# Last image's loads with channels outermost, the second softmax term cast by GpSimd, and scores brought onto pixels by transposes

## The chip, the cores and the metric

The kernel runs on one core of one Trainium2 chip. The metric is device time in microseconds of one execution. Before the change the median of three runs is 5360.88 us (5352.83 to 5364.77).

A core has five engines that run their own instruction queues in order and wait for each other by semaphores: TensorE (PE, with its weight loads listed as PEld), VectorE (DVE), ScalarE (ACT), GpSimd (POOL) and SyncE (SP), which here only issues transfers. TensorE writes to PSUM[...].

## The reference, cut to what matters

The input x is 16 images of 56 x 56 pixels and 384 channels, float32. Two layers follow each other:

```python
x = x + _L0_conv_ref(_gn(x), w_qkv, w_proj, b_proj)   # dilated attention
x = x + _L1_conv_ref(_gn(x), w_conv)                  # depthwise 3x3, binary weights
```

`_gn` is a group norm over 32 groups of 12 channels and a whole image. The attention computes q, k and v with one 384 x 1152 product, and cuts them into 3 groups of 128 channels with dilations 1, 2 and 3. Each group has 4 heads of 32 channels. A pixel attends to its 3 x 3 neighbours at that dilation (9 taps): q times k summed over a head's 32 channels gives 3 x 4 x 9 = 108 scores a pixel, a softmax runs over the 9 taps, and the weights multiply v. A 384 x 384 product and the residual follow. The second layer convolves each channel by itself with weights -1, 0 or 1.

## The kernel before, in words

**Tiling.** An image is cut into 7 chunks of 8 rows, 448 pixels (`PX`), so there are 112 chunks. Inside the kernel a tile holds 128 channels on the partitions and 448 pixels along the free dimension. Images pass through DRAM between stages, channels first: `xd` (the input, transposed) and `x1d` (after the attention).

**Stages.** `plan_a` loads a chunk, transposes it on TensorE (L422), takes statistics and stores it to `xd`. `plan_b` is the attention of one chunk: `normalise`, `k_or_v` and `query` (L463), `score`, the softmax, `turn_weights`, `weigh`, `out_project`. `plan_c` is the convolution and the output of one chunk.

**Order of the work.** The pieces of all plans are entered with `at(when, order, piece)` and then called sorted by time slot and by kind. A chunk advances by `STEP` = 9 slots, so pieces of several chunks and images interleave. The tile framework then schedules the instructions engine by engine, sets the semaphores and gives out the buffers of the pools; nothing else orders the queues. Almost all transfers are issued on SP's queue, in order.

**Scores to softmax.** `score` multiplies q with three shifted copies of k on VectorE (L516, tile `t`). `score_rounds` sums each head's 32 channels by products with a 0/1 matrix (L501), into the PSUM tile `ps`: 27 rounds of 4 rows at scattered places. `softmax_1` copies `ps` to `sT` (ACT, L533) and brings it onto pixels with four matmuls, one for each 112 pixels (L536): `sT` is the stationary operand and `permf`, a 128 x 128 matrix of zeros and ones built at the start (L107), the moving one. It orders the columns by neighbour, and columns 108 to 127 come out as zeros, since only 27 x 4 of its entries are set. Maximum, difference and exponential (L541 to L543), sum, reciprocal and product (L547 to L549) follow.

**Three terms.** The weights `ew` are float32. To carry them through a bfloat16 transposing transfer without loss, they are split in three bfloat16 terms, written in place into `e3`: the first is a cast (ACT, L558), `rest` is what the cast lost (POOL, L559), the second a cast of `rest` (ACT, L563), the third what that lost (POOL, L564). `turn_weights` issues the transposing transfer into `aT` on SP (L569). `weigh` spreads the three terms over the channels by bfloat16 products (L582, tile `pb_a`), VectorE multiplies with v (L589, tile `w`), GpSimd adds up the taps (L597, L600, L601, tiles `w` and `y`), and `out_project` takes `y` through TensorE (L615, tile `po`).

**The last image's convolution.** Its chunks (b = B-1) have no later attention beside them. `load` (L684, L692) fills, for each of two channel groups j, four sets q of 32 channels, each three times on the partitions with rows shifted by one (ky = 0, 1, 2): 96 partitions. The tiles come from the pools `t`, `w` and `xr`, two sets in a tile. For the chunks 1 to 5 one transfer for each q brings all three shifts:

```python
one = by_set[:, q, p0 - W : p0 - W + PX]
three_rows = bass.AP(one.tensor, one.offset, [(W, 3), *one.ap])
nc.sync.dma_start(set_of(j, q), three_rows)
```

The edge chunks 0 and 6, and all other images, use one transfer for each ky (L684). `normalise` (L699, L703) follows, then `convolve` (L717, L724) and `taps_last` (L759), the third group's nine taps on VectorE. `turn` transposes the result (L789), copies it to `osb` (L791, pool `o_p`, two buffers) and stores it (L794), for the last image from ACT's queue.

Of the kernel before, what the change touches and what calls it, by code (L numbers as in the profile page):

```python
# [8 lines left out]
F32 = mybir.dt.float32  # L9
# [8 lines left out]
P = 128  # L18
HEADS = 4
HD = 32  # L20
NG = 3
NTAP = 9
NQ = 4
ROWS = 8
SUB = 112
# [3 lines left out]
NPAD = 32  # L29
# [6 lines left out]
def dilated_attention_then_binary_conv(  # L36
# [28 lines left out]
    nc = tc.nc  # L65
    B, H, W, C = x.shape
    PX = ROWS * W
    NCH = H // ROWS
# [7 lines left out]
    def place(p):  # L76

        g, o = divmod(p, NTAP)
        return NG * o + g
# [22 lines left out]

    perm = const.tile([P, NPAD, HEADS], F32, name="perm")
    nc.gpsimd.memset(perm, 0.0)
    for p in range(NG * NTAP):
        v = place(p)
        nc.gpsimd.affine_select(  # L107
            out=perm[:, v, :], in_=perm[:, v, :], compare_op=ALU.not_equal, fill=1.0,
            base=-(32 * (p % 4) + 4 * (p // 4)), pattern=[[-1, HEADS]], channel_multiplier=1,
        )  # L110
    permf = perm.rearrange("p v h -> p (v h)")
# [39 lines left out]
    y_p = ctx.enter_context(tc.tile_pool(name="y_p", bufs=4))  # L151
# [5 lines left out]
    o_p = ctx.enter_context(tc.tile_pool(name="o_p", bufs=2))  # L157
# [234 lines left out]
    def at(when, order, piece):  # L392

        pieces.setdefault((when, order), []).append(piece)
# [50 lines left out]
    def plan_b(m, t0):  # L445

        b, c = divmod(m, NCH)
# [76 lines left out]
        def by_neighbour(ap):  # L524
            return ap.rearrange("p s (o k) -> p s o k", o=NTAP)

        def over_neighbours(ap):
            return ap.unsqueeze(2).to_broadcast([SUB, NSUB, NTAP, GH])

        def softmax_1():  # L530

            sT = s_p.tile([P, PX], F32, tag="sT", name="sT")
            nc.scalar.copy(sT, had.pop("ps")[:, :PX])  # L533
            pt = ps_mt.tile([P, 512], F32, tag="mt", name="pt_s")
            for s in range(NSUB):
                nc.tensor.matmul(  # L536
                    pt[:SUB, s * P : (s + 1) * P], sT[:, s * SUB : (s + 1) * SUB], permf, start=True, stop=True
                )
            pt4 = pt[:SUB].rearrange("p (s v) -> p s v", s=NSUB)[:, :, :NR]
            mx = s_p.tile([SUB, NSUB, GH], F32, tag="mx", name="mx")  # L540
            nc.vector.reduce_max(mx, by_neighbour(pt4).rearrange("p s o k -> p s k o"), axis=AX.X)  # L541
            nc.vector.tensor_tensor(by_neighbour(weights), by_neighbour(pt4), over_neighbours(mx), ALU.subtract)
            nc.scalar.activation(weights, weights, AF.Exp, scale=SCALE)  # L543
# [8 lines left out]
        e8 = ew.rearrange(EIGHTS, k=8)  # L552
        term = [e3.rearrange("p s u (r k) -> p (s u r) k", r=4)[:, :, 8 * t : 8 * t + 8] for t in range(TERMS)]

        def softmax_3():

            had["rest"] = rest = s_p.tile([SUB, NSUB * NPAD * HEADS], F32, tag="rest", name="rest")
            nc.scalar.copy(term[0], e8)  # L558
            nc.gpsimd.tensor_tensor(rest.rearrange(EIGHTS, k=8), e8, term[0], ALU.subtract)  # L559

        def softmax_4():
            r8 = had["rest"].rearrange(EIGHTS, k=8)
            nc.scalar.copy(term[1], r8)  # L563
            nc.gpsimd.tensor_tensor(term[2], r8, term[1], ALU.subtract)  # L564

        def turn_weights():
# [65 lines left out]
        for i in range(9):  # L632
            at(t0 + i, SCORE, lambda i=i: score(i))
        at(t0 + 9, SOFTMAX, softmax_1)
        at(t0 + 10, SOFTMAX, softmax_2)
        at(t0 + 11, SOFTMAX, softmax_3)
        at(t0 + 12, SOFTMAX, softmax_4)
        at(t0 + 12, LOADS, turn_weights)
        for i in range(9):
            at(t0 + 14 + i, WEIGH, lambda i=i: weigh(i))  # L640
# [4 lines left out]
    def plan_c(m, t0):  # L645

        b, c = divmod(m, NCH)
        p0 = c * PX
        had = {}

        def edges(j):
            found = []
            for z, _, _ in had[f"z{j}"]:
                if c == 0:
                    found.append(z[0:HD, :, 0:W])
                if c == NCH - 1:
                    found.append(z[2 * HD : 3 * HD, :, PX - W : PX])
            return found

        def set_of(j, q):  # L660
            return next(z[:, q - q0] for z, q0, q1 in had[f"z{j}"] if q0 <= q < q1)

        def load(j):
            by_set = x1d[b].rearrange("(j q c) n -> j c q n", q=NQ, c=HD)[j]
            if b < B - 1:
                z = z_p.tile([P, NQ * PX], F32, tag="z", name="z")[:K3].rearrange("p (q n) -> p q n", q=NQ)
                had[f"z{j}"] = [(z, 0, NQ)]
            else:

                had[f"z{j}"] = []  # L670
                for q0 in range(0, NQ, 2):
                    pool, tag = (t_p, "t") if c % 2 == 0 else (w_p, "w") if (j, q0) != (1, 2) else (xr_p, "xr")
                    z = pool.tile([P, 3, PX], F32, tag=tag, name="z_last")[:K3, :2]
                    had[f"z{j}"].append((z, q0, q0 + 2))
            for edge in edges(j):
                nc.gpsimd.memset(edge, 0.0)
            for ky in range(3):
                lo = W if c == 0 and ky == 0 else 0
                hi = PX - W if c == NCH - 1 and ky == 2 else PX
                n0 = p0 + (ky - 1) * W  # L680
                for z, q0, q1 in had[f"z{j}"]:
                    if b == B - 1 and 0 < c < NCH - 1:
                        continue
                    nc.sync.dma_start(  # L684
                        z[ky * HD : (ky + 1) * HD, :, lo:hi], by_set[:, q0:q1, n0 + lo : n0 + hi]
                    )
            if b == B - 1 and 0 < c < NCH - 1:

                for q in range(NQ):
                    one = by_set[:, q, p0 - W : p0 - W + PX]  # L690
                    three_rows = bass.AP(one.tensor, one.offset, [(W, 3), *one.ap])
                    nc.sync.dma_start(set_of(j, q), three_rows)  # L692

        def normalise(j):
            mrz = mr1[b][1]
# [88 lines left out]
        def turn(s):  # L784
            pt = ps_mt.tile([P, 512], F32, tag="mt", name="pt_o")
            mid = had["xg"][:, 1 : ROWS + 1, :].rearrange("p r w -> p (r w)")
            for j in range(NG):
                src = mid if j == JG else had["x1"][:, j]
                nc.tensor.transpose(pt[:SUB, j * P : (j + 1) * P], src[:, s * SUB : (s + 1) * SUB], ident)  # L789
            osb = o_p.tile([SUB, C], F32, tag="osb", name="osb")  # L790
            nc.scalar.copy(osb, pt[:SUB, :C])  # L791

            queue = nc.sync if b < B - 1 else nc.scalar
            queue.dma_start(of[b, p0 + s * SUB : p0 + (s + 1) * SUB, :], osb)  # L794

        if b == B - 1:

            at(t0 - 12, LOADS, load_g)
            at(t0 - 3, LOADS, load_x)
            ahead = 8 if c else 1  # L800
            at(t0 - ahead, NORM, normalise_g)
            for j in range(JG):
                at(t0 - 12 + j, LOADS, lambda j=j: load(j))
                at(t0 - ahead + j, NORM, lambda j=j: normalise(j))
                at(t0 + 1 + j, CONVOLVE, lambda j=j: convolve(j))
            for ky in range(3):
                at(t0 + 1 + ky, CONVOLVE, lambda ky=ky: taps_last(ky))
            for s in range(NSUB):
                at(t0 + 12, STAGE_C, lambda s=s: turn(s))
            return  # L810
# [9 lines left out]
        for j in range(JG):  # L820
            at(t0 - 4 + 3 * j, LOADS, lambda j=j: load(j))
            at(t0 - 1 + 3 * j + late, NORM, lambda j=j: normalise(j))
            at(t0 + 2 + 3 * j + late, CONVOLVE, lambda j=j: convolve(j))
        for s in range(NSUB):
            at(t0 + 9 + s, STAGE_C, lambda s=s: turn(s))

    SOFTMAX, SCORE, STATISTICS, CONVOLVE, WEIGH, QUERY, SPREAD, QKV, PROJECT, STAGE_A, STAGE_C, NORM, LOADS = range(13)
# [43 lines left out]
    for m in range(N):  # L871
        plan_a(m, start_a(m))
        plan_b(m, STEP * m)
        plan_c(m, STEP * (m + 10))
# [31 lines left out]
```

## Time and profile before

| what | value |
|---|---|
| median of three runs | 5360.88 us |
| the profiled execution, its own time | 5362.08 us |
| its span, first to last instruction | 5360.3 us |
| TensorE busy, granted clock | 97%, 0.981 |
| VectorE, ScalarE, GpSimd busy | 78%, 45%, 78% |
| GpSimd adds, L597 | 672 x 3053 ns |
| scores onto pixels on TensorE, L536 | 896 records |
| casts on ScalarE, L558 and L563 | 112 x 618 ns each |
| transfers L692 | 40 of 168 KB |

A row of a group names its line, engine, operation, the written and read tiles, their shapes, the count; then the busy time in us and the mean of one in ns; then the idle time of the engine just ahead of these instructions, and what ended it. TensorE's matmuls are pipelined, so its busy time is not time at its peak, and the mean of one is longer than the distance between two. A row of the timeline gives start, length, engine and the number of instructions merged into it.

### The profile page before, as it was taken

How to read it: one execution, taken by the hardware profiler on the slowest of the kernel's cores; microseconds unless marked ns; L12 is line 12 of the kernel's file. 1: busy time of each engine (PE TensorE's matmuls, PEld its weight loads, DVE VectorE, ACT ScalarE, POOL GpSimd, SP SyncE). 2: the span in 40 equal slices, each digit the busy share in tenths (PEclk: the TensorE clock that was granted, in tenths of full speed). 3: DMA queues.
4: the chain of work that ended last, by engine and by line, in shares of the span. 5: the costliest groups of instructions: out<-in, count | busy, mean ns of one | idle time of the engine just before them, and what ended most of it. 6: DMA issues, size and time to landing. Idle time of an engine off the chain costs nothing.

```text
span 5360.3 us, 76299 instructions
## 1 busy us (share of the span) xinstructions
PE 5174.7 (97%) x27333; PEld 2385.0 (44%) x27333; DVE 4189.1 (78%) x4125; ACT 2400.3 (45%) x4189; POOL 4178.0 (78%) x2839
## 2 busy tenths in 40 slices
PE   8999999999999999999999999999999999999965
PEld 4444444444444444444444444444444444444422
DVE  4887887877888788888888888887788878777754
ACT  3223444444444544444444444544444444444433
POOL 2677888878888888888888888887888888788880
PEclk8999999999999999999999999999999999999976
DMA  6444556655656555555665556655555655444443
GB/s 194 124 116 116 160 163 165 165 153 161 166 157 169 159 163 154 163 155 160 165 165 160 158 160 166 166 157 162 162 154 160 165 157 162 134 129 135 123 130 128
DMA packets 810793, 825.66 MB, mean 154 GB/s; under 512 B 359467, under 2 KB 800174, under 8 KB 810414
## 3 DMA queue, kind: packets, MB, share of 16 engines
q1 hardware_dynamic: 802430, 808.79, 54.9%
q10 hardware_dynamic: 7984, 12.00, 0.7%
q8 instruction: 216, 3.54, 0.3%
q14 instruction: 163, 1.34, 0.1%
HBM read 466.41 MB, written 231.21 MB: 130 GB/s over the span
## 4 chain that ended last, share of the span: by engine, by line
PE 77%; POOL 7%; DVE 7%; DMA 4%; ACT 2%; issue 1%; SPq 1%; POOLq 0%; ACTq 0%; DVEq 0%
PE pkv L463 23%; PE pq L463 13%; PE po L615 11%; PE ps L501 10%; PE pc L717 8%; PE pb_a L582 5%; POOL w L597 3%; DVE t L516 3%; DVE w L589 2%; PE pt_x L422 2%; PE pt_o L789 2%; POOL m L774 2%; PE pt_s L536 1%; ACT m L768 1%; DMA z_last<-x1d 1%
## 5 line engine op out<-in xcount | busy, mean ns | idle before, releaser
L597 POOL TENSOR_TENSOR w<-w 128x1344 f32<-128x1344 f32 x672 | 2051.6, 3053 | 420.6 <-DVE w L589 376.1
L589 DVE TENSOR_TENSOR w<-pb_a,v 128x1344 f32<-128x1344 f32 x1008 | 1558.9, 1547 | 266.6 <-PE pb_a L582 176.7
L516 DVE TENSOR_TENSOR t<-pq,k 128x1344 f32<-128x1344 f32 x1008 | 1536.1, 1550 | 228.9 <-PE pq L463 228.0
L463 PE MATMUL pkv<-xn,wqkvT 128*128 128x448 f32 x3924 | 1569.6, 549 | 11.7 <-ACT osb L791 5.7
L463 PEld LDWEIGHTS pkv<-xn,wqkvT 128*128 128x128 f32 x3924 | 718.4, 190 | 683.2 <-issue 637.5
L774 POOL TENSOR_TENSOR m<-m 128x1344 f32<-128x1344 f32 x210 | 644.5, 3069 | 281.7 <-ACT m L768 281.5
L615 PE MATMUL po<-y,wprojT 128*128 128x448 f32 x2016 | 834.7, 550 | 18.3 <-POOL y L601 14.7
L463 PE MATMUL pq<-xn,wqkvT 128*128 128x448 f32 x1962 | 830.7, 557 | 0.0
L703 ACT ACTIVATE z<-z,mrz 96x448 f32<-96x448 f32 x840 | 578.2, 751 | 360.9 <-DMA z<-x1d 325.3
L501 PE MATMUL ps<-t,sel 128*32 128x448 f32 x6048 | 663.4, 548 | 28.7 <-DVE t L516 28.0
L768 ACT ACTIVATE m<-zg,ktap 128x448 f32<-128x448 f32 x945 | 555.5, 658 | 274.2 <-POOL m L774 267.2
L615 PEld LDWEIGHTS po<-y,wprojT 128*128 128x128 f32 x2016 | 376.6, 192 | 375.8 <-issue 344.0
L717 PE MATMUL pc<-z,kdiag 96*32 96x440 f32 (+1 forms) x5040 | 517.6, 544 | 5.7 <-POOL z L705 4.6
L463 PEld LDWEIGHTS pq<-xn,wqkvT 128*128 128x128 f32 x1962 | 343.9, 189 | 316.9 <-issue 316.9
L601 POOL TENSOR_TENSOR y<-y,w 128x448 f32<-128x448 f32 x336 | 382.0, 1137 | 23.7
L582 PE MATMUL pb_a<-aT,spread 24*128 24x448 bf16 x3024 | 368.6, 359 | 32.5 <-DVE w L589 27.3
L600 POOL TENSOR_TENSOR y<-w 128x448 f32<-128x448 f32 x336 | 382.8, 1139 | 14.5
L618 DVE SCALAR_TENSOR_TENSOR xr<-po,bias,xr 128x448 f32<-128x448 f32 x336 | 227.5, 677 | 202.7 <-PE po L615 197.7
L724 DVE TENSOR_TENSOR x<-pc,x 128x448 f32<-128x448 f32 x224 | 139.1, 621 | 307.3 <-PE pc L717 295.0
L473 ACT COPY v<-pkv 128x448 f32<-128x448 f32 x336 | 178.6, 531 | 448.1 <-PE pkv L463 429.9
L473 ACT COPY k<-pkv 128x448 f32<-128x448 f32 x336 | 178.8, 532 | 401.5 <-PE pkv L463 401.4
L501 PEld LDWEIGHTS ps<-t,sel 128*32 128x32 f32 x6048 | 170.2, 109 | 365.7 <-issue 237.5
(131 smaller groups left out, 4324.0 us busy)
## 6 DMA issues: line engine op xcount, KB each, us to landing
z<-x1d SPq DMA_DIRECT2D x570, 224.0 KB
xr<-xd SPq DMA_DIRECT2D x112, 672.0 KB
x1d<-xr SPq DMA_DIRECT2D x112, 672.0 KB
xn<-xd SPq DMA_DIRECT2D x109, 672.0 KB
xin<-in_x_dram SPq DMA_DIRECT2D x105, 672.0 KB
xd<-xa SPq DMA_DIRECT2D x315, 224.0 KB
out_dram<-osb SPq DMA_DIRECT2D x420, 168.0 KB
x<-x1d SPq DMA_DIRECT2D x112, 448.0 KB
```

Source lines behind the costliest of these rows:

```text
L463: nc.tensor.matmul(dst[:, :PX], wqkvT[:, cc, o0 : o0 + P], had["xn"][:, cc, :], start=(cc == 0), stop=(cc == NG - 1))
L501: return nc.tensor.matmul(had["ps"][32 * j : 32 * j + 32, :PX], sel[:, s0 : s0 + 32], tk, start=(issued[j] == 1), stop=(issued[j] == len(r ...
L516: nc.vector.tensor_tensor(t.rearrange("p k (r w) -> p k r w", w=W), q3, k3, ALU.mult)
L582: return nc.tensor.matmul(pb[:, kx, :PX].rearrange("p (s n) -> p s n", s=NSUB), spread[rows_of, v % 2, :], had["a"][rows_of, :, v // 8, :] ...
L589: nc.vector.tensor_tensor(w.rearrange("p k (r w) -> p k r w", w=W), pb[:, :, :PX].rearrange("p k (r w) -> p k r w", w=W), three(kv[1][g][m ...
L597: nc.gpsimd.tensor_tensor(w0, w0, w, ALU.add)
L600: nc.gpsimd.tensor_tensor(y, w0[:, 0], w0[:, 1], ALU.add)
L615: nc.tensor.matmul(po[:, :PX], wprojT[:, g, j * P : (j + 1) * P], had[f"y{g}"], start=(g == 0), stop=(g == NG - 1))
L703: nc.scalar.activation(z, z, AF.Identity, bias=mrz[:, j, q, 0:1], scale=mrz[:, j, q, 1:2])
L717: return nc.tensor.matmul(pcr[q * HD : (q + 1) * HD, :, lo:hi], kdiag[:, kx, j * NQ + q, :], rows(set_of(j, q))[:, :, lo + kx - 1 : hi + k ...
L768: nc.scalar.activation(rows(t[:, kx]), zp[:, ky : ky + ROWS, kx : kx + W], AF.Copy, scale=ktap[:, o : o + 1])
L774: nc.gpsimd.tensor_tensor(had["m"], had["m"], t, ALU.add)
```

## The change

1. *Scores onto pixels*: the four matmuls with `permf` become four TensorE transposes with `permf` in the identity's place. The matrix gets its last five columns of entries too, so that it is a full permutation: five more selects on GpSimd at the start.
2. *Second term*: the cast of `rest` moves from ScalarE to GpSimd. The softmax's last pieces are cut differently: the first cast stands alone, `rest` becomes a piece of kind PROJECT in the same slot, and cast and third term follow one slot later.
3. *Last image's loads*: chunks 1 to 5 use the form of the others. Instead of four transfers with the three shifts outermost (96 rows each), each channel group takes six (three shifts, two tiles), with 32 channels outermost and two sets inside.
4. *Last image's output tiles* come from `y_p` (four buffers) instead of `o_p` (two).

```diff
-    for p in range(NG * NTAP):
-        v = place(p)
+    for p in range(NPAD):
+        v = place(p) if p < NG * NTAP else p
         nc.gpsimd.affine_select(
...
-                nc.tensor.matmul(
-                    pt[:SUB, s * P : (s + 1) * P], sT[:, s * SUB : (s + 1) * SUB], permf, start=True, stop=True
-                )
+                nc.tensor.transpose(pt[:SUB, s * P : (s + 1) * P], sT[:, s * SUB : (s + 1) * SUB], permf)
...
         def softmax_3():
+            nc.scalar.copy(term[0], e8)
+
+        def softmax_4():
             had["rest"] = rest = s_p.tile([SUB, NSUB * NPAD * HEADS], F32, tag="rest", name="rest")
-            nc.scalar.copy(term[0], e8)
             nc.gpsimd.tensor_tensor(rest.rearrange(EIGHTS, k=8), e8, term[0], ALU.subtract)
 
-        def softmax_4():
+        def softmax_5():
             r8 = had["rest"].rearrange(EIGHTS, k=8)
-            nc.scalar.copy(term[1], r8)
+            nc.gpsimd.tensor_copy(term[1], r8)
             nc.gpsimd.tensor_tensor(term[2], r8, term[1], ALU.subtract)
...
-        at(t0 + 12, SOFTMAX, softmax_4)
+        at(t0 + 11, PROJECT, softmax_4)
+        at(t0 + 12, SOFTMAX, softmax_5)
...
                 for z, q0, q1 in had[f"z{j}"]:
-                    if b == B - 1 and 0 < c < NCH - 1:
-                        continue
                     nc.sync.dma_start(
                         z[ky * HD : (ky + 1) * HD, :, lo:hi], by_set[:, q0:q1, n0 + lo : n0 + hi]
                     )
-            if b == B - 1 and 0 < c < NCH - 1:
-
-                for q in range(NQ):
-                    one = by_set[:, q, p0 - W : p0 - W + PX]
-                    three_rows = bass.AP(one.tensor, one.offset, [(W, 3), *one.ap])
-                    nc.sync.dma_start(set_of(j, q), three_rows)
...
-            osb = o_p.tile([SUB, C], F32, tag="osb", name="osb")
+            if b < B - 1:
+                osb = o_p.tile([SUB, C], F32, tag="osb", name="osb")
+            else:
+                osb = y_p.tile([P, PX], F32, tag="y", name="osb_last")[:SUB, :C]
```

## The prediction

> **What bounds the kernel now.** I read the engine shares and the chain first, then the groups of instructions, then the order of time inside one chunk, and last the transfers of the end, where the slices look different. The page:
>
> ```profile
> span 5360.3 us, 76299 instructions
> PE 5174.7 (97%) x27333; PEld 2385.0 (44%) x27333; DVE 4189.1 (78%) x4125; ACT 2400.3 (45%) x4189; POOL 4178.0 (78%) x2839
> ...
> PE 77%; POOL 7%; DVE 7%; DMA 4%; ACT 2%; issue 1%; SPq 1%; POOLq 0%; ACTq 0%; DVEq 0%
> ```
>
> TensorE carries 77% of the chain. In windows of 2000 us from the middle it is busy 1986 and 1985 us at full clock, VectorE 1612 and GpSimd 1645. A chunk (448 pixels, 112 of them) takes 45.4 us there: PE is the bound of the loop, with some 20% air on VectorE and GpSimd. A microsecond taken off PE counts; one added to GpSimd counts only if something waits for it.
>
> The groups that the change touches, and their neighbours:
>
> ```profile
> L422 PE MATMUL pt_x<-ident,xin 112*128 112x112 f32 x1260 | 181.1, 268 | 16.7 <-DMA xin<-in_x_dram 16.7
> L559 POOL TENSOR_TENSOR rest<-ew,e 112x512 f32<-112x512 f32 x112 | 130.0, 1160 | 167.0 <-ACT e L558 167.0
> L564 POOL TENSOR_TENSOR e<-rest,e 112x512 bf16<-112x512 f32 x112 | 129.8, 1159 | 1.5 <-ACT e L563 1.5
> L536 PE MATMUL pt_s<-perm,sT 128*112 128x128 f32 x896 | 116.5, 273 | 1.6 <-ACT sT L533 1.5
> L563 ACT CAST e<-rest 112x512 bf16<-112x512 f32 x112 | 69.2, 618 | 229.3 <-POOL rest L559 229.3
> L173 POOL MEMSET ew<- 112x512 f32 x1 | 0.5, 514 | 0.0
> ```
>
> The counts are the point: L536 is 112 chunks x 4 matmuls = 448, and the trace holds 896, two per matmul. L422 is 105 chunks x 12 transposes = 1260, one each. The 273 ns overlap, so the price is read from the order of time (start, length, engine):
>
> ```profile
> 2530.02 1.04 PE L536 MATMUL pt_s<-perm,sT 128*112 128x128 f32 x8
> ...
> 2530.99 0.36 PE L582 MATMUL pb_a<-aT,spread 24*128 24x448 bf16 x3
> ...
> 2535.89 0.55 PE L422 MATMUL pt_x<-ident,xin 112*128 112x112 f32 x4
> ```
>
> Eight records in 1.04 us with a last one of 0.27: (1.04-0.27)/7 = 0.11 us apart. Four transposes of 112 columns: (0.55-0.27)/3 = 0.093 us apart, 0.107 for 128 columns.
>
> The end of the kernel is another stage: after about 5216 us only the last image's convolution is left. Its transfers (40 slices of 5262 to 5302 us), SP's issues, and the busy times of 5216 to 5316 (PE, PEld, DVE, ACT, POOL, clock, DMA share, GB/s):
>
> ```profile
> GB/s 252 121 207 85 75 74 78 212 78 205 85 75 76 75 77 77 77 75 75 75 203 229 75 76 76 113 323 296 156 75 75 100 194 76 73 86 214 77 76 74
> ...
> 5261.39 23.21 SPq L692 DMA_DIRECT2D z_last<-x1d  x10
> ...
> 5216.00:5316.00 100.00, 57.71 (x366) 20.14 (x366) 37.25 (x67) 35.18 (x57) 3.74 (x20) 0.60 0.37 122
> ```
>
> The rate lies on a floor of 75 GB/s, a quarter of the 323 GB/s that the same window reaches, while no compute engine is 60% busy: the loads of L692 are the bound. They are 40 x 168 KB = 6.88 MB, 92 us at 75 GB/s; the first is issued at 5215.8 and the last at 5315.3.
>
> **What the Trainium skill says.** "DMA: Bandwidth & Descriptors", Rules for kernel authors: the number of DMA engines of a transfer follows the slowest dimension of its patterns, and an outermost dimension under 16 confines the transfer to that many engines. L692's source has 3 rows outermost; 75 is 3 x 25 GB/s, so the trace agrees. "TensorE: Matmul & The Clock Gate", Terms: the transpose mode is 4x faster for FP32. The trace shows half the records at equal spacing, 2x; I use that. "GPSIMD Engine Reference", 3.1: two-operand work costs about 2.6 cycles an element, one-operand work as little as 1.8, with 769 ns measured for 512 elements. The 1160 ns of L559 agrees with the first; no copy runs on GpSimd in this trace.
>
> **The change part by part.** *Transposes*: 4 records fewer of 0.11 us per chunk, 0.44 x 112 = 49 us of PE. The built program keeps PE's order (98% of its instructions keep their place), so nothing else moves there. PE's idle time is about 1% of the loop, and its waits are mostly for answers to its own results (products from pq to the ps matmuls, evictions of its PSUM tiles), which come earlier with it. I take 44 us; ends 15 (VectorE's or ScalarE's answers pin the cycle) and 55 (all of it, and ScalarE's freed time). The five added selects on the matrix cost 5 x 0.2 = 1 us of GpSimd at the start.
>
> *The cast*: ScalarE loses 0.62 us and the 2.05 us (229.3/112) that it stood waiting for rest, with pt_x and pt_o evictions queued behind. GpSimd gains one copy, 0.51 (the memset) to 1.16 us (the two-operand row); I take 0.77. Its 37.3 us a chunk become 38.1 of 45.4. Where it stands matters more. Before: sum over taps (w), rest, w, third term, y, y. After: w, w, rest, y, cast, y, third term. From the end of the first w, with the second w of 3.05 in both: before, 3.05+1.16+1.16 = 5.4 plus 1.26 waiting for the first cast = 6.6; after, 3.05 plus up to 0.8 waiting for VectorE's product, 1.16+1.14+0.77+1.14+1.16 = 9.2. VectorE's softmax division also moves behind one 1.55 us product; the second w covers that. So the third term ends about 3 us later, and with it the transposing transfer. Queued behind that on SP are loads of z, stores of x and of the result, then xg. Are they needed sooner?
>
> ```profile
> 2545.07 1.55 SPq L569 DMA_TRANSPOSE aT<-e  x1
> ...
> 2554.84 0.36 PE L582 MATMUL pb_a<-aT,spread 24*128 24x448 bf16 x3
> ```
>
> From issue to first use are 9.8 us here (median of 90 chunks 10.1, least 7.7); the transfer's 256-byte packets end 3.5 us after the issue (at most 4.9). Slack: 6.5 median, 4.2 least. The 3 us are hidden. On SP one z load moves ahead of the transposing transfer, and SP idles 1.1 and 0.4 us a little later waiting for evictions, so xg comes about 1.6 us later, ScalarE's normalisations 1.5 to 2.3 later; the eviction of v behind them (2561.56) was 3.0 us ahead of the PE group that needs its bank (about 2565.1). Cost 0, at worst 0.5 us a chunk, which is inside my 15.
>
> *Tail loads*: the same 6.88 MB become 60 transfers of 32 channels x 2 x 448, 16 engines wide. What binds next, per chunk of the last image: VectorE 9 x 0.68 + 2 x 0.51 + 2 x 0.62 = 8.4; ScalarE 6 x 0.755 + 0.84 + 4 x 0.47 + 4 issues x 0.32 = 8.5; transfers 2.8 MB at 300 GB/s = 9.4; SP 12 x 0.42 + 0.8 = 5.9; PE 6.8 at full clock (2 x 2.4 + 4 x 0.5), 12 at the 0.6 granted now (2 x 4.65 + 4 x 0.68). They share buffers, so the largest is a floor; I take 11. The first chunk ends at about 5237 today and isn't touched; 6 x 11 = 66 gives 5303, and 6 us for the last transposes, copies and stores (now four output tiles instead of two) give 5309. Against 5360.3: 51 us. Ends: 8.7 a chunk, 65 us; 15 a chunk, 27 us.
>
> Sum: 5360.3 - 44 - 51 + 1 = 5266; the profiled execution was 5362.1 us in all, 1.2 over the median of the runs, so I say 5265.
>
> **Rivals.** (a) *Both gains arrive*, 5265: chance 0.66. (b) *The loop keeps its pace*: the saved PE time turns into waits for VectorE (the ps matmuls wait 28.0 us for t, pb_a 27.3 us for w already). For: VectorE and ScalarE answer some PE groups with 0.05 to 0.3 us to spare. Against: 20% air on both. 5360 - 15 - 45 = 5300: 0.14. (c) *The tail finds another bound at once*: the clock stays at 0.6 and PE needs 12 us a chunk, with hand-overs 15. For: 0.60 granted there. Against: denser work is what brought the clock back between 5230 and 5236 us. 5360 - 44 - 27 = 5289: 0.11. (d) *The transposes are issued as two records still*, only the tail gains: 5310. Against: L422 and L789 are float32 and single. 0.02. (e) *Slower*: the cast makes aT late. Place: SP's wait at L569 and the first pb_a of each chunk. It decides when the delay passes the slack of 6.5 us; each further microsecond costs 112 us. To eat both gains (95 us) the delay must be 7.4 us instead of 3, a cast of 5 us; at 6 us the kernel ends at 5380. Against: 4 times the dearest row of that size. 0.05. The last 0.02 is no change.
>
> **How the numbers follow.** The likeliest case is (a). Its own span is 15 to 55 and 27 to 65, both ends rarely together: 5240 to 5300. (b) and (c) lie mostly inside; the range 5238 to 5306 leaves (d), (e), part of (b) and a better loop outside, some 2 in 10. About 0.2% (11 us) is what a measurement here can tell from no change; (a) to (d) are all faster than that: 0.93, same 0.02, slower 0.05.
>
> **What would show it.** L536's line with 448 records and about 0.43 us a group; a period near 45.0; a CAST on GpSimd of 0.5 to 1.2 us, ScalarE's 229 us wait gone, no PE wait for aT; in the tail no floor at 75 GB/s, and 10 to 12 us from chunk to chunk. Wrong if PE waits for aT or for evictions appear every chunk, if the copy takes over 2 us, or if the tail stays on one transfer.

## The result, and the profile after

The changed kernel takes 5432.5 us (5423.9 to 5437.5), the kernel before 5357.0 in the same session. The estimated ratio of the two is 1.0133, interval 1.0122 to 1.0145, which is 65 to 78 us; the medians are 75 us apart. The kernel is slower, where the prediction said 5265, which is 96 us faster than the 5361 that it started from. Its profiled execution spans 5428.7 us. First the page of the changed kernel:

```profile
span 5428.7 us, 75442 instructions
...
PE 5152.7 (95%) x26885; PEld 2341.1 (43%) x26885; DVE 4183.3 (77%) x4125; ACT 2316.2 (43%) x4077; POOL 4252.4 (78%) x2956
```

TensorE is busy 22 us less than before and yet the span is 68 us longer: its idle time grew. The groups that were changed, with the softmax division (L548) among them (busy time, mean ns of one, idle time before them):

```profile
L565 POOL TENSOR_TENSOR e<-rest,e 112x512 bf16<-112x512 f32 x112 | 129.6, 1158 | 0.1
L560 POOL TENSOR_TENSOR rest<-ew,e 112x512 f32<-112x512 f32 x112 | 129.4, 1155 | 63.6 <-ACT e L556 63.6
L548 DVE TENSOR_TENSOR ew<-ew,sm 112x432 f32<-112x432 f32 x112 | 92.8, 829 | 0.0
L564 POOL CAST e<-rest 112x512 bf16<-112x512 f32 x112 | 68.0, 607 | 0.2
L537 PE MATMUL pt_s<-perm,sT 128*112 128x128 f32 x448 | 67.6, 273 | 4.5 <-ACT sT L534 4.4
```

Everything that the edits say of themselves has arrived: 448 records at L537 where there were 896, a copy of 0.61 us on GpSimd, ScalarE's wait for rest gone. So the loss lies in what they moved. The middle of the loop, first before, then after (columns as in the prediction: behind the length of the window stands TensorE's busy time), and two waits of TensorE (us in total, times, longest), before and after:

```profile
600.00:2600.00 2000.00, 1985.92 (x10644) 918.32 (x10637) 1611.83 (x1565) 947.76 (x1656) 1644.93 (x1057) 1.00 0.59 161
600.00:2600.00 2000.00, 1939.64 (x10201) 879.29 (x10199) 1573.79 (x1531) 897.85 (x1582) 1635.33 (x1076) 0.99 0.57 157
```

```profile
PE ps L501 <- DVE t L516: 28.0, 41, 1.7
PE pb_a L582 <- DMA aT<-e: 3.1, 2, 2.5
```

```profile
PE ps L502 <- DVE t L517: 80.1, 85, 1.7
PE pb_a L583 <- DMA aT<-e: 60.8, 20, 4.0
```

TensorE is busy 1940 of 2000 us instead of 1986. The score matmuls wait 52 us more for the products t, and pb_a waits 58 us more for the transposed weights aT. From the scores of chunk 7 to those of chunk 104 a chunk takes 46.75 us instead of 45.73: 98.5 us in all, 7.1 us an image. The seven chunks of an image don't share it evenly: from the third one's pt_s to the next takes 3.7 us longer, the first 2.1, the last 1.4, the fourth is 1.5 us shorter, the others lose 0.2 to 0.6.

Where aT gets late is seen in the order of time (start, length). The third chunk of the ninth image, before:

```profile
2716.89 3.06 POOL L597 TENSOR_TENSOR w<-w 128x1344 f32<-128x1344 f32 x1 [2.18 <-DVE w L589]
...
2719.50 0.92 DVE L549 TENSOR_TENSOR ew<-ew,sm 112x432 f32<-112x432 f32 x1
...
2719.90 3.42 POOL L774 TENSOR_TENSOR m<-m 128x1344 f32<-128x1344 f32 x1
2723.40 2.35 POOL L779 TENSOR_TENSOR m<-m 128x448 f32<-128x448 f32 x2
2725.71 1.17 POOL L559 TENSOR_TENSOR rest<-ew,e 112x512 f32<-112x512 f32 x1
...
2727.93 1.16 POOL L564 TENSOR_TENSOR e<-rest,e 112x512 bf16<-112x512 f32 x1
...
2729.12 1.56 SPq L569 DMA_TRANSPOSE aT<-e  x1
```

and the same chunk after, 59.3 us later at its first line:

```profile
2776.19 3.07 POOL L598 TENSOR_TENSOR w<-w 128x1344 f32<-128x1344 f32 x1 [2.19 <-DVE w L590]
2779.23 3.04 POOL L768 TENSOR_TENSOR m<-m 128x1344 f32<-128x1344 f32 x1
...
2780.62 2.12 DVE L548 TENSOR_TENSOR ew<-ew,sm 112x432 f32<-112x432 f32 x1
...
2782.35 1.39 POOL L773 TENSOR_TENSOR m<-m 128x448 f32<-128x448 f32 x1
2783.70 3.06 POOL L598 TENSOR_TENSOR w<-w 128x1344 f32<-128x1344 f32 x1
2786.73 1.14 POOL L773 TENSOR_TENSOR m<-m 128x448 f32<-128x448 f32 x1
2787.83 1.13 POOL L601 TENSOR_TENSOR y<-w 128x448 f32<-128x448 f32 x1
2788.93 1.16 POOL L560 TENSOR_TENSOR rest<-ew,e 112x512 f32<-112x512 f32 x1
...
2791.13 0.61 POOL L564 CAST e<-rest 112x512 bf16<-112x512 f32 x1
...
2792.80 1.16 POOL L565 TENSOR_TENSOR e<-rest,e 112x512 bf16<-112x512 f32 x1
...
2793.98 1.55 SPq L570 DMA_TRANSPOSE aT<-e  x1
...
2798.06 0.56 PE L583 MATMUL pb_a<-aT,spread 24*128 24x448 bf16 x3 [3.97 <-DMA aT<-e]
```

Counted from the first line, the division starts 1.8 us later (another product now stands ahead of it on VectorE) and lasts 2.12 us instead of 0.92, so it ends 3.0 us later. It ends 0.47 us after the long m sum on GpSimd (a sum of the convolution), which it met; more of that below. In GpSimd's new order the second sum over taps stands ahead of rest, so rest comes 3.9 us later, the third term 5.6, aT 5.6. TensorE stands still for 4.0 us. Of the 20 waits for aT, 14 are in the third chunk of an image. How the new order makes the products t late was not followed in this way.

The end of the kernel is no longer slowed by its loads in the same measure. The 40 slices of the whole span, before and after:

```profile
GB/s 194 124 116 116 160 163 165 165 153 161 166 157 169 159 163 154 163 155 160 165 165 160 158 160 166 166 157 162 162 154 160 165 157 162 134 129 135 123 130 128
GB/s 192 131 104 112 160 163 153 161 155 159 158 159 152 155 159 154 161 159 160 156 152 155 157 161 161 155 161 156 156 165 153 154 152 160 146 132 132 130 128 155
```

The last slice moves 155 GB/s instead of 128; a window inside that stage follows with the tail's experiments.

### The profile page after: what moved, and what is told of

It is laid out like the page before. It is cut to its first block, busy times and chain, and to the rows that moved or that the text cites. A ratio compares the mean times of both kernels' runs of the same rounds, so it can differ in the third digit from the quotient of the medians.

```text
span 5428.7 us, 75442 instructions
## 1 busy us (share of the span) xinstructions
PE 5152.7 (95%) x26885; PEld 2341.1 (43%) x26885; DVE 4183.3 (77%) x4125; ACT 2316.2 (43%) x4077; POOL 4252.4 (78%) x2956
## 5 line engine op out<-in xcount | busy, mean ns | idle before, releaser
L464 PE MATMUL pq<-xn,wqkvT 128*128 128x448 f32 x1962 | 860.0, 574 | 0.0
L583 PEld LDWEIGHTS <-spread 24*128 24x128 bf16 x3024 | 100.9, 91 | 577.8 <-issue 497.6
```

Source lines behind the costliest of these rows:

```text
L464: nc.tensor.matmul(dst[:, :PX], wqkvT[:, cc, o0 : o0 + P], had["xn"][:, cc, :], start=(cc == 0), stop=(cc == NG - 1))
L583: return nc.tensor.matmul(pb[:, kx, :PX].rearrange("p (s n) -> p s n", s=NSUB), spread[rows_of, v % 2, :], had["a"][rows_of, :, v // 8, :] ...
```

## The experiments

Two theories stood at the start. *Order*: an edit re-sorted VectorE's and GpSimd's queues, and the new order is what costs. *Cast*: the copy on GpSimd makes the third term and aT late (the prediction's rival e), and the transposes save what they promised. A third question was how much the tail gives.

### Each edit alone

The transposes with the completed matrix, as in the diff above, and nothing else:

> Only the scores' transposes (with the completed permutation matrix), the rest as before. The built program shows that this edit alone re-sorts the queues: the softmax division goes behind one more product on VectorE, the rest (the subtraction after the first cast) behind the second sum over taps on GpSimd. Order theory: this new order is what the loop lost, so about 5357 + 106 = 5460 us (5420 to 5480), TensorE waiting for the transposed weights (aT) and for the products t. Cast theory (the copy on GpSimd makes aT late, the transposes save what they promised): 5357 - 45 = 5312 us (5300 to 5330).

Measured 5464.7 us, ratio 1.0196 (1.0181 to 1.0212). The cast and the cut of the softmax pieces, and nothing else:

> Only the second cast on GpSimd and the softmax cut in five pieces, the rest as before. In the built program the orders on TensorE and VectorE are exactly those of before, GpSimd's is the old one with the copy right behind rest. Order theory: the slack of aT hides it, 5357 us with at most 15 to either side. Cast theory: the copy costs the loop some 106 + 45 = 150 us, so about 5505 us.

Measured 5413.2 us, ratio 1.0095 (1.0080 to 1.0110). The two tail edits:

> Only the two edits of the tail (loads with channels outermost, four output tiles), the rest as before. Both theories: the loop as before and a tail some 31 us shorter, as read from the two traces: 5326 us (5315 to 5335). The prediction's sum said 51 us: 5306.

Measured 5318.3 us, ratio 0.9924 (0.9907 to 0.9940); kernel before 5361.6. For the transposes the order theory's 5460 is met and the cast theory's 5312 fails. For the cast alone both fail: it is not free, as the order theory had it, and at 52 us it is far from the cast theory's 150. The tail lies inside the range expected, 12 us above the prediction's sum.

What the transposes' edit does to the order stands in the built programs, and VectorE's rows are found again in the traces. Number of chunks, of 112, with each sequence (SUM: sum of the softmax, REC: reciprocal, DIV: division, stats: statistics of x, T2: third term):

```
                                  before  cast alone  transposes alone  changed
VectorE  SUM t REC stats DIV          83          83                 1        1
VectorE  SUM t stats REC w DIV         1           1                96       96
GpSimd   rest ahead of second sum     83          83                 0        0
```

The cut of the softmax into five pieces, with the cast left on ScalarE, moves no instruction on any engine. So the new order comes from the transposes alone: the layer that sorts the queues places them otherwise than matmuls. Why it does was not looked into. The transposes alone have their stall in another place than the changed kernel. A group of ScalarE and a wait of TensorE in the run with the transposes alone:

```profile
L562 ACT CAST e<-rest 112x512 bf16<-112x512 f32 x112 | 69.3, 619 | 413.8 <-POOL rest L558 413.7
...
PE pkv L464 <- ACT xa L435: 55.0, 12, 4.6
```

ScalarE waits 414 us for the late rest instead of 229, the eviction xa stands behind that cast, and TensorE waits for the eviction in 12 chunks of the kind shown above. With the cast on GpSimd this wait goes, and aT is late instead.

### Order and transposes taken apart

For the next runs the order of one built program is written into another kernel, as a list of moves per engine (shortened here):

```diff
+    for queue, moves in ((nc.tensor, ORDER_PE), (nc.vector, ORDER_DVE), ...):
+        order = [own[queue.engine][k + move] for k, move in enumerate(moves)]
+        for before, after in zip(order, order[1:]):
+            tc.add_manual_dep(after, before.name, <issue order only>, reason="order")
```

Here own holds the recorded instructions of each engine. The transposes in the old order, and the old products in the transposes' order:

> The transposes, but with the instructions of every engine held in the order of the kernel before (the order of the built program before is written into the kernel as edges that only order the issue). Order theory: the transposes then save their 0.44 us a chunk, 5357 - 45 = 5312 us (5300 to 5325). A theory that the transposes themselves are what slows the loop (their results later, or the matrix's padding): no gain, 5357 or more. Cast theory: the same as the transposes alone, 5312.

> The converse: the kernel before with its products kept (no transposes), every engine held in the order that the kernel with the transposes alone was built with. If the order alone is what costs: the transposes alone took 5465 and their own saving was 25 us in the old order, so 5465 + 25 = 5490 us (5475 to 5520). If the transposes are needed for the loss (their results arriving at another moment, the matrix): 5362, as before.

Measured 5337.0 (ratio 0.9954, 0.9939 to 0.9969) and 5467.3 us (1.0200, 1.0185 to 1.0216). Both lie outside what was expected, 12 us above 5300 to 5325 and 8 below 5475 to 5520, but with the kernel before and the transposes alone they are four corners: old order 5361 with products, 5337 with transposes; new order 5467 with products, 5465 with transposes. The order costs 106 to 128 us whichever way the scores are turned. The transposes save 25 us in the old order and nothing that can be measured in the new one. In the old order pt_s takes 0.53 us instead of 0.97, as predicted, but not all of it arrives: in many images the period falls by the whole 0.44 us in five of the seven chunks, but in nearly all not at all in the third, and in the fourth it swings by up to 3 us either way. ps waits 41.5 us for t, before 28.0; the loop's period falls by 0.26 us.

Which queue is the root? VectorE alone was held, in both directions:

> The transposes, with VectorE alone held in the order of before; the other queues as the scheduler then makes them: GpSimd has rest again ahead of the second sum in 83 chunks and differs from before only at 12 chunks and small work. If VectorE's division behind a product is the root: 5337 to 5350 us, nearly all of the loss gone. If the remaining differences on GpSimd, ScalarE, SyncE and TensorE matter by themselves: 5400 or more.

> The kernel before with its products, VectorE alone held in the order that the transposes' edit gave it; in the built program GpSimd follows by itself (rest behind the second sum in all but a few chunks). Root theory: the whole loss, 5467 us (5445 to 5480). If GpSimd's, ScalarE's and SyncE's own re-sorting carries a good part: 5380 to 5440.

Measured 5375.3 us (1.0030, 1.0019 to 1.0042) and 5481.1 us (1.0224, 1.0209 to 1.0239). VectorE's order alone brings the whole loss, 14 us more than with all five queues and 1 us above its range; GpSimd follows by itself. Giving VectorE its old order takes back 89 of the 128 us. It reaches neither of the two expectations; 38 more come with the differences on the other four engines. These runs move VectorE's whole order; the last run below changes only the priority of the reciprocal and the division.

### The cast

First the changed kernel with the cast given back to ScalarE, `nc.scalar.copy(term[1], r8)` for `nc.gpsimd.tensor_copy(term[1], r8)`, and the pieces of the softmax cut as before:

> The changed kernel with the cast given back to ScalarE: transposes and both tail edits, in the order that the scheduler makes of them. If the tail's gain is the same in the new order: 5465 - 43 = 5422 us, and the cast's own share in the changed kernel is then only some 10 us, since the late rest no longer stands in ScalarE's way. Cast theory of the prediction's failure: 5281. If the tail's gain shrinks in the new order to the 31 us read from the traces: 5434, and the cast costs nothing there.

Measured 5421.7 us (1.0116, 1.0101 to 1.0131). The tail's gain is 43 us in the new order too (5464.7 - 5421.7), and in the changed kernel the cast costs 5432.5 - 5421.7 = 11 us, about the least that two sessions can tell apart. The six runs that follow ask why it costs 52 alone. In the first of them the copy is placed behind the second sum (only the list of GpSimd's order differs from the run with the cast alone); the copy's time is put on GpSimd without its place in the softmax, by one added line,

```diff
             nc.gpsimd.tensor_tensor(term[2], r8, term[1], ALU.subtract)
+            nc.gpsimd.tensor_copy(spare.rearrange(EIGHTS, k=8), r8)
```

the cast stands in the old queues of the others; and the new queues of ScalarE and SyncE stand alone, without the cast:

> The cast on GpSimd as in the run with the cast alone, the other four engines in the same order as there; on GpSimd the copy stands directly ahead of the third term, which in 83 chunks puts it behind the second sum over taps instead of ahead of it. Place theory (the copy ahead of the sum holds the w buffer and VectorE's next product): most of the 52 us are gone, 5362 to 5380. Time theory (0.6 us more of GpSimd a chunk, wherever): 5413. Chain theory (the third term later, aT later): 5413 or more, with TensorE waiting for aT.

> The kernel before, every engine held in its order, plus one copy of the size of the cast (112 x 512 to bf16, 0.61 us) on GpSimd into a spare tile that nobody reads, directly behind the third term; ScalarE keeps its cast. So GpSimd's time alone, outside the way of the softmax. Time theory (GpSimd 0.6 us a chunk later with its sums; VectorE's softmax division, which in the traces ends 0.466 us after the end of the sum it meets, then waits longer): about 5362 + 50 = 5410 us, and the division's mean rises from 0.91 to 1.2 us. Theory that what costs is the cast's place on the way from rest to aT, or the queues of ScalarE and SyncE that the edit re-sorted: 5362.

> The cast on GpSimd directly behind rest, every other engine held in the order of before (ScalarE's without its 112 casts; the edit as built had moved 15 more instructions on ScalarE and 70 on SyncE). Time theory: 5410 us, as the cast alone. Queue theory (SyncE's and ScalarE's new order is the cost): 5362 to 5375.

> The kernel before, cast on ScalarE, but ScalarE's and SyncE's queues in the order that the cast's edit gave them (65 loads of z behind two more stores on SyncE, 15 normalisations later on ScalarE). If this order costs by itself: 5361 + 27 = 5388 us. If it costs only with the copy on GpSimd: 5361.

Measured 5409.7 (1.0093), 5368.2 (1.0014, 1.0007 to 1.0021), 5386.2 (1.0047, 1.0032 to 1.0062) and 5359.8 us (1.0002, 0.9993 to 1.0010). The place theory falls: behind the sum it costs the same. The chain theory falls as well: with the cast alone TensorE waits 9.9 us for aT in all, before 3.1. The time theory falls: 0.61 us of GpSimd a chunk outside the softmax cost 8 us in all, and the division's mean even fell to 0.86 us. With the other engines held in their old queues the cast costs 26 us, half of what it costs with the new ones; the new queues of ScalarE and SyncE cost nothing by themselves.

What the traces of the three runs with a dear cast share is a longer division (mean 1.19 to 1.22 us). The group before, and with the cast alone:

```profile
L549 DVE TENSOR_TENSOR ew<-ew,sm 112x432 f32<-112x432 f32 x112 | 102.3, 913 | 0.4
```

```profile
L549 DVE TENSOR_TENSOR ew<-ew,sm 112x432 f32<-112x432 f32 x112 | 136.7, 1220 | 0.4
```

VectorE stands 34 us longer in it. One by one the divisions are of two kinds: before, 49 take 0.58 to 0.64 us and 63 take longer, and each of these 63 ends 0.46 to 0.48 us after the end of the GpSimd sum that was running when it started. With the cast alone 93 do so. The Trainium skill has a reason, in "SBUF — State Buffer", section "SBUF: two separate sides": a VectorE operation with two SBUF inputs and a GpSimd operation that reads SBUF share one pair of ports, and whichever starts first holds it to its end. So one input was taken out of SBUF, into PSUM, the memory that TensorE writes to:

```diff
-            nc.vector.reciprocal(sm, sm)
-            nc.vector.tensor_tensor(by_neighbour(weights), by_neighbour(weights), over_neighbours(sm), ALU.mult)
+            inv = ps_mt.tile([P, 512], F32, tag="mt", name="inv")[:SUB, : NSUB * GH].rearrange(...)
+            nc.vector.reciprocal(inv, sm)
+            nc.vector.tensor_tensor(by_neighbour(weights), by_neighbour(weights), over_neighbours(inv), ALU.mult)
```

> The kernel before with one thing changed: the reciprocal of the softmax sums is written to a PSUM tile, so the division reads only one of its inputs from SBUF. Lock theory: the division never waits for GpSimd's sums, its mean falls from 0.91 to about 0.6 us and VectorE gains 36 us, of which some reach TensorE: 5325 to 5360 us; TensorE may lose a little by the third PSUM bank being held. If the long divisions come from something else, the mean stays at 0.9.

> The same with the cast on GpSimd; TensorE's and VectorE's orders are those of the run beside it. If the cast's cost goes through the division: 0 to 20 us more than that run. If not: 45 to 55 us more, as without the change to PSUM.

Measured 5411.9 (1.0094, 1.0079 to 1.0109) and 5419.0 us (1.0109, 1.0092 to 1.0126). The group in the first of them:

```profile
L550 DVE TENSOR_TENSOR ew<-ew,inv 112x432 f32<-112x432 f32 x112 | 65.7, 586 | 0.0
```

No division is long any more: the meeting with GpSimd was the cause of the long ones. And the cast then costs 7 us instead of 52. The first run is itself 51 us slower than the kernel before, where 1 to 36 us faster was expected. The long divisions can't be the reason; which it is was not taken apart: inv takes one of the three buffers of ps_mt, and the edit re-sorts the queues in places. Most of it is in the third chunk of each image, whose period rises from 47.6 to 49.9 us. In the other six chunks of an image the period is within 0.5 us of the kernel before, and summed over these six the cast adds -0.1 us, where alone it added 1.9; in the third chunk it adds 0.8 instead of 1.6. So in six chunks of seven the cast's cost goes through the division that meets GpSimd, as far as a kernel with other queues can show it. In the third chunk TensorE then waits for aT: 13.6 us in 16 waits, without the cast 1.5 in two. Why the re-sorted queues double the cost stays open. It also fits that in the changed kernel, where the cast is nearly free, the division has the same mean with it, 0.83 us, as without it, 0.84.

### The tail's two edits, and a faster kernel

The loads without the tiles, and the tiles without the loads, each as in the diff above:

> Only the loads of the last image with channels outermost, output tiles as before. The prediction gave the whole 51 us of the tail to the loads, with the output tiles worth nothing by themselves; the two together measured 43 us. If the loads are all of it: 5318 us. If waits for the two output tiles (their store had ended most of the waits of pt_o) then bind: 5325 to 5340.

> Only the output tiles of the last image taken from the pool of y (four instead of two), loads as before. The loads' floor stays, so 5361 us; if the stores' waits were on the path, 5345 to 5355.

Measured 5321.7 (0.9930, 0.9915 to 0.9944) and 5357.4 us (0.9997, 0.9988 to 1.0006). The loads are the gain, 36 us by themselves; the tiles alone do nothing, and with the loads (0.9924) they cannot be told from the loads alone. The window of the last stage with both tail edits (columns as in the prediction):

```profile
5216.00:5296.00 80.00, 56.00 (x438) 29.92 (x430) 53.40 (x89) 41.23 (x69) 2.08 (x9) 0.77 0.66 186
```

186 GB/s instead of 122, VectorE 67% busy instead of 37%, TensorE's clock 0.77 instead of 0.60. No single engine is full. On TensorE the convolution products (pc) of one chunk follow those of the one before after 12.6 to 13.5 us.

Two kernels join what gained, without the cast: one with the lists of the old order, one with two lines under raised priority instead:

```diff
-            nc.vector.reciprocal(sm, sm)
-            nc.vector.tensor_tensor(by_neighbour(weights), by_neighbour(weights), over_neighbours(sm), ALU.mult)
+            with tc.high_priority():
+                nc.vector.reciprocal(sm, sm)
+                nc.vector.tensor_tensor(by_neighbour(weights), by_neighbour(weights), over_neighbours(sm), ALU.mult)
```

> The transposes and both tail edits, without the cast, every engine held in the order that the tail edits alone were built with (the loop in the order of before). If the two gains are independent: 5337 - 43 = 5294 us (5283 to 5303), faster than both kernels. If the tail's gain needs the old pace of the loop, or is only 31 us as in the changed kernel: 5306.

> A short form of the repair: transposes and both tail edits, no cast, and the reciprocal and the division of the softmax traced with raised priority, without a list of orders. In the built program rest stands ahead of the second sum again in 84 chunks and the division ahead of the product in 97. Between the run with all orders held (5297) and that with VectorE's alone (5375 - 43 = 5332): 5297 to 5335 us, faster than both kernels.

Measured 5297.0 us (0.9882, 0.9867 to 0.9896) and 5343.0 us (0.9970, 0.9960 to 0.9980). Both beat both kernels; the first is 135 us faster than the changed one. The second missed its range by 8 us. Against the same kernel without the raised priority (5421.7 us, with the cast on ScalarE) it gains 79 us, so where these two instructions stand on VectorE, with what moves along with them, is most of the loss. It is 46 us behind the full order; what of the order it lacks was not taken apart. Its division is long again (mean 1.19 us, with the full order 0.96), as it is in the run with VectorE alone held (1.21 against 0.91), which was 38 us behind; whether that is the reason was not tested.

## Why the prediction was wrong, step by step

*What bounds the kernel*: right. TensorE carried the loop, and 20% air on VectorE and GpSimd did not keep a delay there from reaching it.

*Transposes*: the saving at pt_s was right (448 records, 0.44 us a chunk), and 25 us of the 44 taken arrive when nothing else moves, inside the 15 to 55 given. The step that failed is in the part on the cast: "VectorE's softmax division also moves behind one 1.55 us product; the second w covers that." The move was seen, but put down to the cast, while it belongs to the transposes, and it was priced at nothing. The order that it is part of makes the transposes alone 103 us slower than the kernel before. In the chunk shown the second sum does not cover a late rest; it stands in front of it. "So nothing else moves there" spoke of TensorE alone, and the loss came in by the queues that feed it.

*Cast*: its length, 0.61 us, lay between the bounds given, below the 0.77 taken. "The third term ends about 3 us later" was 5.6 us in the chunk that stalls, and that chunk is the one of the least slack, 4.2, so "the 3 us are hidden" was false there: TensorE waits 4.0 us, since it also comes to that product 2.0 us sooner after its pt_s than before. "Cost 0, at worst 0.5 us a chunk" had its worst end met by the cast alone (52 / 112 = 0.46); in the changed kernel it is 11 / 112 = 0.10. The queue on SyncE, priced at nothing, is free by itself, but together with ScalarE's it doubles the price of the copy.

*Tail*: the mechanism was right and the size off: 43 us instead of 51, inside 27 to 65. The term that was short is the pace of a chunk, about 13 us instead of 11. Six chunks at 2 us would be 12 us; the shortfall is 8, so the other terms were a little too dear.

*The rivals*: (e) named the place, the wait for aT, and was given 0.05 because only the copy's length was weighed, not where the neighbours stand in the queues. (b), a saving that turns into waits for t, is what the transposes do in the new order, where ps waits 76 us for t instead of the 42 with the products. In (e) one figure does not follow: at 112 us for each further microsecond a cast of 6 us would end near 5460, not at 5380. The sum of the parts as measured is 103 - 43 + 11 = 71 us, against 75 for the whole; the 11 is itself the difference that the other two leave, so the sum shows no more than that they add up.

## What to carry to other kernels

Where a layer sorts the queues, build each edit alone and compare the order of every engine, not only of the one that bounds: here exchanging four matmuls for four transposes moved the softmax division behind one product in 96 of 112 chunks, and the new order outweighed everything the edits were for. Price a moved instruction by what then stands in front of its successors on the next engine's queue, chunk kind by chunk kind, since the largest loss, 3.7 us, came in one chunk of seven and the next one gained 1.5. And if a saving on the bounding engine is to count, hold the order of the kernel before when measuring it.

## What the runs showed of the hardware

A VectorE product of two SBUF tensors (112x432, float32) takes 0.59 us alone. If it meets a running GpSimd sum of two SBUF tensors it ends 0.46 to 0.48 us after that sum's end: all 63 long ones before, which last up to 2.7 us. The other way round, the m sum shown above that starts while a division runs takes 3.42 us instead of 3.05. With one input in PSUM the mean is 0.586 us and none of the 112 takes over 0.61, though 101 start beside a running GpSimd instruction. That the two exclude each other is what the page of the skill named above says, and the traces agree; the 0.46 to 0.48 us are measured here. A float32 transpose of a 128x112 block through a permutation matrix gives one record where a matmul gives two, and four of them take 0.44 us less (0.53 instead of 0.97). A copy of 112x512 from float32 to bf16 takes 0.61 us on GpSimd and 0.62 on ScalarE.
